# Pauses in the indexed transfers beside the first sorted tiles, and a PSUM tile for the last gates' values

## The chip, the core and the metric

The kernel runs on one core of a Trainium2 chip. The metric is the device time of one execution in microseconds (us); lower is better. Engines: PE (TensorE: matrix products and transposes), DVE (VectorE), ACT (ScalarE), POOL (GpSimd), SP (which issues most of the DMAs). SBUF is the working memory of 128 partitions, PSUM the small memory into which PE writes.

## What is computed

The input is `x`, four images of 32 x 128 x 128. Layer 0 groups pixels two by two, so that each image becomes a matrix `q` of 128 channels by 4096 positions:

```python
energy = einsum('bci,bcj->bij', q, q)          # 4096 x 4096 per image
energy = energy / (d_i * d_j)                  # d: root of the diagonal
out = gamma * einsum('bcj,bij->bci', q, softmax(energy)) + xs
```

Layer 1 sees each image as tokens of 128 values (4096 per image): a layer norm and a linear attention without softmax, added to the tokens, then a second layer norm and a mixture of eight experts, of which each token takes the best two:

```python
t = t + attention(ln(t))
probs = softmax(ln(t) @ router_w + router_b)
top_p, top_i = top_k(probs, 2); top_p /= sum(top_p)
t = t + sum_k top_p[k] * (ln(t) @ expert_w[top_i[k]] + expert_b)
```

## The kernel before

**Layer 0.** Images b = 0 to 3 follow each other in `attend` (L415). PE multiplies blocks of 128 x 512 of the normed `q` (L556), ACT takes the exponential (L559), PE multiplies the result with `q` transposed (L440). The matrix is symmetric, so a block's transpose serves the mirrored place; it is made by DVE, written to DRAM and read back by SP's DMAs (`blocks`, `G`), and used at L375 to L385. This loop fills PE for most of the time.

**Layer 1 as a stream.** The tokens of an image lie in SBUF as 32 rows of 128 tokens (`T`, `xn`: partition, row, value). `layer1(b)` returns generators whose every `yield` is one step. The main loop at the bottom walks through `attend`; it keeps a list `steady` and gives each stream in it one step every PACE = 10 units of the attention's clock, so layer 1 of image b runs inside the attention of image b + 1. On PE, DVE, ACT and SP the program's own order is kept (a manual schedule); an instruction that waits holds what stands behind it on its engine. POOL's power and indexed transfers are pinned in program order too.

For b = 0 to 2 a stream is `all_parts`: `close_rows` (ends layer 0's rows and makes the first norm's statistics, L690 on), `matrix` (the attention's small products), and `attention_rows`, which ends in `sorted_experts(h)` (L933 on) for the 16 rows of each half h. This sorts the tokens by expert:

- 32 indexed transfers, *scatters* (L989, issued by POOL), put each token's normed values at two places of a list `xs` in DRAM, two transfers per two steps. Half 1 starts its scatters when half 0's are issued (`turns[0]` has "moved").
- the list is read in pairs of tiles of 128 tokens by SP's DMAs (L1013, into `bufs`), transposed by PE (L1056), evicted by ACT (L1023), multiplied by the expert's weights on PE (L1049), evicted by DVE (L1032) and written to `ys` in DRAM (L1035).
- 32 indexed transfers, *gathers* (L1114, POOL), read the results back by token; DVE weighs and adds them (`combine`, L1083), SP stores the result. Half 0 gathers after half 1's scatters are issued, half 1 after half 0 gathered.

So half 1's scatters and half 0's first tiles are issued in the same steps. The first step of the next image's closing, `close_rows(0)`, waits until the stream before has finished its tiles (`st["sorted"]`).

**The last image.** After the attention there is nothing to hide behind. `last_parts` (L1186 on) therefore computes all eight experts for each token without sorting: two products of 128 x 512 per row k (L1198), DVE multiplying some experts by their gates and adding (`scaled_sums`, L1141), ACT scaling the others (`scaled_rows`, L1155; `by_scalar(k)` gives ACT 6 of 8 for k < 8, 5 for k < 14, else 4), POOL summing those (`sum_rows`, L1163 to L1167). The loop over k runs 32 + 4 times; each pass issues the products for row k + 2, and then one step of `rest`, the generator `second_half`: statistics of rows 16 to 31 (`close_stats`, L625 to L640), router (`router_rows`, L806 on), gates (`route(1)`, L821 on), normalising on ACT (L644) and transposes (`transpose_tokens`: PE L870, ACT copy L866). Rows 0 to 15 are routed before the loop; there the rows 8 to 15 are normalised and transposed too (8 ACT operations and tiles 2 and 3, before `for k`). Ahead of the loop stand `close_stats` of rows 0 to 15 with POOL's power `pow_neg_half` (L164), named `rsa` or `rsf` by its result.

PSUM's eight banks are shared out as two for `pe`, one `po`, two `pg`, three `pt` (`psum_t`).

Of the kernel before, what the change touches and what calls it, by code (L numbers as in the profile page):

```python
# [16 lines left out]
ALU = mybir.AluOpType  # L17
AX = mybir.AxisListType
# [4 lines left out]
def kernel(  # L23
# [43 lines left out]
    nc = tc.nc  # L67
# [11 lines left out]
    E = router_w.shape[1]  # L79
# [18 lines left out]
    def psum_t(name):  # L98
        return ps_t.tile([P, CH], F32, tag="pt", name=name)
# [6 lines left out]
    rank = const.tile([P, 1, E], F32, tag="rank", name="rank")  # L106
# [5 lines left out]
    rb_sb = const.tile([P, 1, E], F32, tag="rb", name="rb_sb")  # L112
# [3 lines left out]
    srw = const.tile([P, 1, E], F32, tag="srw", name="srw")  # L116
# [61 lines left out]
    def idle(n):  # L178
        for _ in range(2 * n):
            yield  # L180
# [421 lines left out]
    def layer1(b, st):  # L602
# [5 lines left out]
        rsf, nbf, nbo = (stat.tile([P, KT, 1], F32, tag=nm, name=f"{nm}_{b}", bufs=1) for nm in ("rsf", "nbf", "nbo"))  # L608
        lg = stat.tile([P, KT, E], F32, tag="lg", name=f"lg_{b}", bufs=1)
# [5 lines left out]
        gate = first  # L615
# [26 lines left out]
        def normalise(rows, rs, nb):  # L642
            for k in rows:
                nc.scalar.activation(xn[:, k, :], T[:, k, :], AF.Identity, scale=rs[:, k, :], bias=nb[:, k, :])  # L644
# [158 lines left out]
                    bank[:, ts(j - j0, D + 2 * E)], keep[k // 4][:, ts(k % 4, P)], matx, start=True, stop=True  # L803
                )

        def router_rows(eng, r0, nr, la):  # L806

            sh = [P, nr, E]
            rows = slice(r0, r0 + nr)
            w1, w2 = (stat.tile([P, 16, E], F32, tag=nm, name=f"{nm}_{b}_{r0}", bufs=1)[:, :nr] for nm in ("lw1", "lw2"))  # L810
            eng.tensor_tensor(w1, nba[:, rows].to_broadcast(sh), srw.to_broadcast(sh), ALU.mult)
            eng.tensor_tensor(w1, la[:, :, E:], w1, ALU.subtract)
            eng.tensor_tensor(w1, w1, sda[:, rows].to_broadcast(sh), ALU.mult)
            eng.tensor_tensor(w1, w1, la[:, :, :E], ALU.add)
            yield
            eng.tensor_tensor(w2, nbf[:, rows].to_broadcast(sh), srw.to_broadcast(sh), ALU.mult)
            eng.tensor_tensor(w2, w2, rb_sb.to_broadcast(sh), ALU.add)
            eng.tensor_tensor(w1, w1, rsf[:, rows].to_broadcast(sh), ALU.mult)
            eng.tensor_tensor(lg[:, rows], w1, w2, ALU.add)

        def route(h):  # L821

            sh = [P, KT // 2, E]
            rows = slice(h * KT // 2, (h + 1) * KT // 2)
            ms, dn = (stat.tile([P, KT // 2, 1], F32, tag=nm, name=f"{nm}_{b}_{h}") for nm in ("ms", "dn"))
            pr = stat.tile(sh, F32, tag="prob", name=f"prob_{b}_{h}", bufs=1)
            mx = weight[:, 1, rows]
            o1, o2 = first[:, rows], second[:, rows]
            v = lg[:, rows]
            nc.vector.tensor_reduce(mx, v, AX.X, ALU.max)  # L830
            nc.vector.tensor_tensor(pr, v, mx.to_broadcast(sh), ALU.subtract)
            nc.scalar.activation(pr, pr, AF.Exp)
            yield
            nc.vector.scalar_tensor_tensor(o1, pr, 1.0, rank.to_broadcast(sh), ALU.is_equal, ALU.mult)
            nc.vector.tensor_reduce(ms, o1, AX.X, ALU.max)
            nc.vector.tensor_tensor(o1, o1, ms.to_broadcast(sh), ALU.is_equal)
            nc.vector.scalar_tensor_tensor(pr, o1, -2.0, pr, ALU.mult, ALU.add)
            yield
            nc.vector.tensor_reduce(mx, pr, AX.X, ALU.max)
            nc.vector.tensor_tensor(o2, pr, mx.to_broadcast(sh), ALU.is_equal)  # L840
            nc.vector.tensor_tensor(o2, o2, rank.to_broadcast(sh), ALU.mult)
            nc.vector.tensor_reduce(ms, o2, AX.X, ALU.max)
            yield
            nc.vector.tensor_tensor(o2, o2, ms.to_broadcast(sh), ALU.is_equal)
            nc.vector.tensor_scalar(dn, mx, 1.0, None, ALU.add)
            nc.vector.reciprocal(dn, dn)
            if not alone:
                nc.vector.tensor_copy(weight[:, 0, rows], dn)
                nc.vector.tensor_tensor(mx, mx, dn, ALU.mult)
                return  # L850
            nc.vector.tensor_tensor(o2, o2, mx.to_broadcast(sh), ALU.mult)
            nc.vector.tensor_tensor(o1, o1, o2, ALU.add)
            nc.vector.tensor_tensor(gate[:, rows], o1, dn.to_broadcast(sh), ALU.mult)

        def add_rows(u, j0, la, pa):
            nj = min(3, 8 - j0)
# [5 lines left out]
        def transpose_tokens(g, alloc=psum_t):  # L862

            pt, done = hold(
                f"ptf_{b}_{g}",
                lambda p: nc.scalar.activation(xn[:, ts(g, 4), :], p.rearrange("p (j t) -> p j t", t=P), AF.Copy),  # L866
                alloc,
            )
            for j in range(4):
                nc.tensor.transpose(pt[:, ts(j, P)], xn[:, 4 * g + j, :], ident)  # L870
            return done
# [42 lines left out]
        def sorted_experts(h):  # L914


            sh = [P, HR, E]
            pad = HR // 2
            r0 = HR * h
            half = slice(r0, r0 + HR)  # L920
            o1, o2 = first[:, half], second[:, half]
# [65 lines left out]
            for n in range(2 * HR):  # L987
                k, i = r0 + n // 2, n % 2
                inst = nc.gpsimd.indirect_dma_start(xs[h], offset(place[:, i, k : k + 1]), xn[:, k, :], None)  # L989
                if not scatters:  # L990
                    pinned(inst)
                else:
                    tc.declare_no_dep(inst.ins, group=f"scatter_{b}_{h}", reason="no two tokens have the same place")
                tc.add_to_no_dep_group(f"scatter_{b}_{h}", inst.ins)
                wait_for(inst.ins, xs_made[h] + xs_read[h], "what is replaced was made and read before")
                wait_for(inst.ins, exps, "not more of these at a time than steps have")
                scatters.append(inst.ins)
                if n % 2:
                    yield
                    yield  # L1000
            turns[h].append("moved")
            xs_made[h][:], xs_read[h][:] = scatters, []
            yield from idle(3)
# [104 lines left out]
            for n in range(2 * HR):  # L1108
                k, i = r0 + n // 2, n % 2
# [59 lines left out]
        def store(g):  # L1169
            for s in range(2):  # L1170
                for r1 in range(2):
                    p0 = s * 64 + r1 * 32
                    nc.sync.dma_start(dst[s, r1, :, ts(g, 4), :], accs[g][p0 : p0 + 32])
# [9 lines left out]
        def last_parts():  # L1183
# [53 lines left out]
            def second_half():  # L1237

                bs, stats = batch_stats("f", 16, 16)
                for u in (2, 3):  # L1240
                    tg = T[:, ts(u, 8), :]
                    nc.vector.tensor_tensor(tg, tg, copies[u], ALU.add)
                    yield
                    for j in range(8):
                        stats[8 * u - 16 + j]()
                        if j % 4 == 3:
                            yield
                close_stats("f", 16, 16, bs)
                yield
                logits = router_rows(nc.vector, 16, 16, la[:, 16:])  # L1250
                next(logits)
                yield
                yield
                for _ in logits:
                    pass
                gates = route(1)
                next(gates)
                yield
                for g in range(4, 8):
                    normalise(range(4 * g, 4 * g + 4), rsf, nbo)  # L1260
                    next(gates, None)
                    yield
                    transpose_tokens(g)()
                    yield
# [10 lines left out]
            gates = route(0)  # L1275
# [4 lines left out]
                pass  # L1280
            products = [product(k, h, bank(f"py_{b}_{k}_{h}")) for k in range(2) for h in range(2)]
            transpose_tokens(1)()
            normalise(range(8, 16), rsf, nbo)
            transpose_tokens(2)()
            transpose_tokens(3)()
            for k in range(KT + 4):
                if k < KT:
                    n = by_scalar(k)
                    scaled_sums(k, products[:2], 8 - n)
                    scaled_rows(k, products[:2], n)  # L1290
                    products = products[2:]
                    if k + 2 < KT:
                        products += [product(k + 2, h, bank(f"py_{b}_{k + 2}_{h}")) for h in range(2)]
                if 1 <= k <= KT and k % 2 == 0:
                    sum_rows(k // 2 - 1, by_scalar(k - 2), nc.vector if k == KT else nc.gpsimd)
                if k >= 5 and k % 4 == 1:
                    store(k // 4 - 1)
                if k >= 1:
                    next(rest, None)

# [102 lines left out]
```

## Time and profile before

| | |
|---|---|
| three runs | 1736.75, 1737.0, 1741.14 us; median 1737.0 |
| profiled execution | 1730.18 us, of which the span of its instructions is 1728.4 |
| granted PE clock, mean | 0.989 |
| scatters L989 | 192, mean 0.969 us on POOL; 510.9-611.3, 924.5-1021.9, 1330.9-1428.3 |
| gathers L1114 | 192, mean 0.966 us; 660.0-772.3, 1072.6-1180.4, 1477.9-1583.1 |
| combines L1083 of image 2 | until 1588.9 |
| loop over k of the last image | about 1652.4 to 1723.4, last store landed at 1728.4 |

The profile records one execution. Its times count from the start of the span. A row of a timeline reads: start, duration, engine, line, operation, output<-inputs, shapes, how many in a row, and in brackets the idle time of the engine before it with what ended it ("<-ACT xn L1023": that instruction of ACT). Durations of L989 and L1114 are POOL's issuing; the transfer itself goes on in the DMA queues. A window table gives each engine's busy time within the stretch.

### The profile page before, as it was taken

Reading aid. Unit: us, or ns where it says so; the run is one execution under the profiler, and the core shown is the slowest. Engines: PE = TensorE matmul, PEld = TensorE weight load, DVE = VectorE, ACT = ScalarE, POOL = GpSimd, SP = SyncE. Lnnn points to the kernel's source line nnn. Section 1 sums busy time; section 2 is a strip of 40 time slices with the busy share of each in tenths; the row PEclk is TensorE's granted clock in tenths of the full one; section 3 lists DMA queues with packets and bytes.
Section 4 is the critical chain, followed back from the end, with each engine's and each line's share of the span. In section 5 each row is a group of like instructions: output and inputs, shape, how many; then the busy total and the mean of one; then the engine's idle time right before and its main releaser. Section 6 shows DMA issues by size and latency. Waiting matters only on the chain. (4 is left out here: it accounts for less than half of the span.)

```text
span 1728.4 us, 21211 instructions
## 1 busy us (share of the span) xinstructions
PE 1656.8 (96%) x5458; PEld 876.9 (51%) x5458; DVE 939.3 (54%) x2443; ACT 925.8 (54%) x2893; POOL 511.8 (30%) x553
## 2 busy tenths in 40 slices
PE   7999999999999999989999999999999999999887
PEld 4444444455554456445564455545555445544633
DVE  4433334367485235467568334557748524455686
ACT  3555445465565455446565544546656545545376
POOL 1000000011026514550014631652102650453156
PEclk9999999999999999989999999999999999999999
DMA  4775778876569899996568979998656988995001
GB/s 128 202 206 170 205 208 238 250 213 183 158 195 271 241 259 262 246 257 182 168 189 228 277 230 262 283 252 231 183 163 196 269 242 260 269 259 135 1 13 38
DMA packets 240681, 355.25 MB, mean 206 GB/s; under 512 B 27312, under 2 KB 155312, under 8 KB 226480
## 3 DMA queue, kind: packets, MB, share of 16 engines
q1 hardware_dynamic: 220048, 314.91, 64.5%
q0 software_dynamic: 12288, 25.19, 4.9%
q10 hardware_dynamic: 8224, 13.77, 2.8%
q8 instruction: 46, 0.75, 0.2%
q14 instruction: 75, 0.61, 0.1%
HBM read 183.64 MB, written 173.15 MB: 206 GB/s over the span
## 5 line engine op out<-in xcount | busy, mean ns | idle before, releaser
L559 ACT ACTIVATE pr<-pe 128x512 f32<-128x512 f32 (+1 forms) x576 | 322.4, 560 | 557.0 <-PE pe L556 428.8
L440 PE MATMUL po<-pr,qT 128*128 128x512 f32 (+3 forms) x1152 | 552.9, 562 | 3.9 <-ACT o L445 3.4
L375 PE MATMUL pg<-G,qT 128*128 128x512 f32 x880 | 453.4, 597 | 14.1 <-DMA G<-blocks 8.7
L556 PE MATMUL pe<-qn,qn 128*128 128x512 f32 x896 | 462.5, 598 | 3.3 <-ACT pr L559 3.0
L369 DVE STREAM_TRANSPOSE F<-pr 128x512 f32<-128x512 f32 x440 | 306.1, 702 | 156.1 <-ACT pr L559 132.1
L440 PEld LDWEIGHTS po<-pr,qT 128*128 128x128 f32 x1152 | 216.6, 191 | 251.8 <-issue 224.4
L380 ACT ACTIVATE junk<-G 128x512 bf16<-128x512 f32 x440 | 273.0, 621 | 7.1 <-DMA G<-blocks 7.0
L375 PEld LDWEIGHTS pg<-G,qT 128*128 128x128 f32 x880 | 167.5, 192 | 214.0 <-issue 187.0
L1114 POOL DMA_INDIRECT yb<-ys,place x192 | 185.5, 966 | 262.5 <-DMA xn<-xs 96.3
L989 POOL DMA_INDIRECT xs<-xn,place x192 | 186.1, 969 | 132.2 <-ACT pr L559 55.3
L556 PEld LDWEIGHTS pe<-qn,qn 128*128 128x128 f32 x896 | 155.3, 192 | 115.9 <-issue 103.0
L385 DVE TENSOR_TENSOR o<-o,pg 128x512 f32<-128x512 f32 x110 | 75.5, 686 | 203.1 <-PE pg L375 164.6
L164 POOL TENSOR_TENSOR rn<-ss,neg_half 128x8 f32<-128x8 f32 (+1 forms) x17 | 26.9, 1586 | 334.1 <-DVE ss L325 334.1
L559 ACT ACTIVATION_READ_ACCUMULATOR pr<-pe 128x1 f32 x576 | 112.1, 195 | 0.0
L1023 ACT ACTIVATE xn<-pys 128x256 f32<-128x256 f32 (+1 forms) x120 | 45.0, 377 | 118.3 <-PE pys L1056 67.7
L1049 PEld LDWEIGHTS pys<-ew_sb,xn 128*128 128x128 f32 x468 | 68.5, 192 | 56.3 <-issue 39.0
L164 POOL TENSOR_TENSOR rsf<-dm_f,neg_half 128x8 f32<-128x8 f32 (+1 forms) x15 | 26.2, 1748 | 233.7 <-DVE sv_f L636 233.7
L556 PE MATMUL pe<-qn 128*128 128x512 f32 (+3 forms) x256 | 91.1, 438 | 0.7 <-ACT qn L344 0.7
L164 POOL TENSOR_TENSOR rsa<-dm_a,neg_half 128x8 f32<-128x8 f32 x16 | 26.4, 1650 | 219.3 <-DVE sv_a L636 219.0
L380 ACT ACTIVATION_READ_ACCUMULATOR junk<-G 128x1 f32 x440 | 84.4, 192 | 0.0
L1049 PE MATMUL pys<-ew_sb,xn 128*128 x468 | 72.1, 277 | 11.1 <-ACT xn L1023 11.0
L1032 DVE COPY result<-pys 128x256 f32<-128x256 f32 (+1 forms) x60 | 24.6, 411 | 96.5 <-ACT xn L1023 48.7
(189 smaller groups left out, 1607.6 us busy)
## 6 DMA issues: line engine op xcount, KB each, us to landing
blocks<-F SPq DMA_DIRECT2D x108, 1024.0 KB
G<-blocks SPq DMA_DIRECT2D x432, 256.0 KB
xn<-xs SPq DMA_DIRECT2D x114, 128.0 KB
below<-F SPq DMA_DIRECT2D x31, 384.0 KB
G<-below SPq DMA_DIRECT2D x124, 96.0 KB
out_dram<-acc SPq DMA_DIRECT2D x128, 64.0 KB
xx<-in_x_dram SPq DMA_DIRECT2D x62, 128.0 KB
ys<-xn SPq DMA_DIRECT2D x60, 128.0 KB
```

The costliest lines, as they stand in the source:

```text
L164: pinned(nc.gpsimd.tensor_tensor(dst, src, neg_half.to_broadcast(list(src.shape)), ALU.pow))
L369: f()
L375: nc.tensor.matmul(pg.rearrange("p (a f) -> p a f", a=4), st["qT"][i][:, ib, :], G[:, :, ib], start=(ib == 0), stop=(ib == NJ - 1),)
L380: nc.scalar.activation(junk, G[:, :, ib], AF.Copy, accum_out=st["sums"][:, NJ * i + ib, jc : jc + 1])
L385: nc.vector.tensor_tensor(o, o, pg.rearrange("p (a j c) -> p a j c", a=4, c=S), ALU.add)
L440: nc.tensor.matmul(row["po"][:, lo:hi], qT[blk // NJ][:, blk % NJ, :], w, start=start, stop=(row["left"] == 0))
L556: nc.tensor.matmul(pe[:, c0:], qn[jc][:, ts(j, P)], qn[i][:, c0:], start=True, stop=True)
L559: nc.scalar.activation(pr[:, c0:], pe[:, c0:], AF.Exp, accum_out=sums[:, t, i : i + 1]).ins
L989: inst = nc.gpsimd.indirect_dma_start(xs[h], offset(place[:, i, k : k + 1]), xn[:, k, :], None)
L1023: nc.scalar.activation(bufs[4 + g % 2][:, :n], p[:, : n * P].rearrange("p (j t) -> p j t", t=P), AF.Copy)
L1049: nc.tensor.matmul(p[:, 2 * P + j * D : 2 * P + j * D + D], bufs[4 + g % 2][:, j, :], weights[:, bass.ds(begins[2 * (g % 2) + j], D)], sta ...
L1114: inst = nc.gpsimd.indirect_dma_start(yb[k // 4][:, i, k % 4, :], None, ys, offset(place[:, i, k : k + 1]))
```

## The change

1. In `sorted_experts`, half 1's scatters pause for `idle(2)`, which is four steps, after each eighth of the transfers n = 7, 15 and 23.
2. In the last image, `router_rows` and `route` take an optional PSUM tile `temps` of [128, 4, 16, 8], one `pt` bank. Rows 16 to 31 keep their intermediates there: one product, one sum and the logits (places 0 and 1), and in `route` the logits, the rank values, the probabilities and the second choice (0 to 3). About 20 DVE operations have at least one operand in PSUM instead of SBUF; the exponential's in and out lie there as well. Statistics, `dn` and the weights stay in SBUF.
3. The eight normalises of rows 8 to 15 and the transposes of tiles 2 and 3 move from before the loop over k into its passes 0 to 7: one row per pass, a tile's transposes and copy at passes 3 and 7, after that pass's products, scaled rows and sums, and before its step of `rest`.

The counts of instructions stay the same on PE, DVE and POOL.

```diff
-        def router_rows(eng, r0, nr, la):
+        def router_rows(eng, r0, nr, la, temps=None):
...
+            w0, sums = w2, lg[:, rows]
+            if temps is not None:
+                w1, w0, sums = temps[:, 0], temps[:, 1], temps[:, 0]
...
-            eng.tensor_tensor(w2, nbf[:, rows].to_broadcast(sh), srw.to_broadcast(sh), ALU.mult)
-            eng.tensor_tensor(w2, w2, rb_sb.to_broadcast(sh), ALU.add)
+            eng.tensor_tensor(w0, nbf[:, rows].to_broadcast(sh), srw.to_broadcast(sh), ALU.mult)
+            eng.tensor_tensor(w2, w0, rb_sb.to_broadcast(sh), ALU.add)
             eng.tensor_tensor(w1, w1, rsf[:, rows].to_broadcast(sh), ALU.mult)
-            eng.tensor_tensor(lg[:, rows], w1, w2, ALU.add)
-
-        def route(h):
+            eng.tensor_tensor(sums, w1, w2, ALU.add)
+
+        def route(h, temps=None):
...
+            ranks = o1
+            if temps is not None:
+                v, ranks, pr, o2 = (temps[:, n] for n in range(4))
...
-            nc.vector.tensor_tensor(o1, o1, o2, ALU.add)
-            nc.vector.tensor_tensor(gate[:, rows], o1, dn.to_broadcast(sh), ALU.mult)
+            nc.vector.tensor_tensor(o2, o1, o2, ALU.add)
+            nc.vector.tensor_tensor(gate[:, rows], o2, dn.to_broadcast(sh), ALU.mult)
...
                 if n % 2:
                     yield
                     yield
+                if h == 1 and n % 8 == 7 and n < 28:
+                    yield from idle(2)
...
-                logits = router_rows(nc.vector, 16, 16, la[:, 16:])
+
+                temps = psum_t("gates").rearrange("p (n k e) -> p n k e", n=4, e=E)
+                logits = router_rows(nc.vector, 16, 16, la[:, 16:], temps)
...
-                gates = route(1)
+                gates = route(1, temps)
...
-            normalise(range(8, 16), rsf, nbo)
-            transpose_tokens(2)()
-            transpose_tokens(3)()
...
+                if k < 8:
+                    normalise(range(8 + k, 9 + k), rsf, nbo)
+                    if k % 4 == 3:
+                        transpose_tokens(2 + k // 4)()
```

In `route` the rank operations use `ranks` in place of `o1` for their intermediate; `o1` itself stays in SBUF.

More of the change, by code (lines that the diff above doesn't have):

```diff
@@ L833, in route @@
             yield
-            nc.vector.scalar_tensor_tensor(o1, pr, 1.0, rank.to_broadcast(sh), ALU.is_equal, ALU.mult)
-            nc.vector.tensor_reduce(ms, o1, AX.X, ALU.max)
-            nc.vector.tensor_tensor(o1, o1, ms.to_broadcast(sh), ALU.is_equal)
+            nc.vector.scalar_tensor_tensor(ranks, pr, 1.0, rank.to_broadcast(sh), ALU.is_equal, ALU.mult)
+            nc.vector.tensor_reduce(ms, ranks, AX.X, ALU.max)
+            nc.vector.tensor_tensor(o1, ranks, ms.to_broadcast(sh), ALU.is_equal)
             nc.vector.scalar_tensor_tensor(pr, o1, -2.0, pr, ALU.mult, ALU.add)
```

## Prediction

> **What bounds the kernel now.** I read the page's shares first, then its chain of waits, then the timeline of the last 80 us, the timelines and windows around the first sorted tiles, and last how the change reorders each engine's instructions.
>
> ```profile
> PE 1656.8 (96%) x5458; PEld 876.9 (51%) x5458; DVE 939.3 (54%) x2443; ACT 925.8 (54%) x2893; POOL 511.8 (30%) x553
> ```
>
> TensorE is busy 1656.8 of 1728.4 us. What a change can give is among the 72 us in which it isn't, or where it stretches behind others. The chain has nothing but PE's lines at its head, so the question is local: where does PE stand still beside the edited lines? First place, the first sorted tiles of rows 0 to 15, in each of the batches 0 to 2 (batch 1 shown; the number in brackets is the engine's idle time before, with its releaser):
>
> ```profile
> 996.40 0.96 POOL L989 DMA_INDIRECT xs<-xn,place  x1 [0.30 <-issue]
> 999.48 0.39 ACT L1023 ACTIVATE xn<-pys 128x256 f32<-128x256 f32 x1 [6.50 <-remote]
> 999.91 0.71 PE L1049 MATMUL pys<-ew_sb,xn 128*128 x4 [3.36 <-ACT xn L1023]
> 1000.71 0.96 POOL L989 DMA_INDIRECT xs<-xn,place  x1 [3.35 <-ACT pr L559]
> ```
>
> The scatters run every 1.26 us (0.96 and 0.30 of issue) until 997.4. The first eviction of transposed tiles (L1023) then starts 6.50 us late, and the product behind it holds PE, in order, for 3.36 us. Two-microsecond windows (columns: length, busy time and count of PE, PEld, DVE, ACT, POOL, then PE clock, DMA share, GB/s):
>
> ```profile
> 991.00:993.00 2.00, 2.00 (x6) 0.95 (x5) 0.00 (x0) 1.45 (x5) 1.39 (x3) 1.00 1.01 423
> ...
> 995.00:997.00 2.00, 1.55 (x4) 0.38 (x2) 0.00 (x0) 0.00 (x0) 1.56 (x2) 1.00 0.21 72
> 997.00:999.00 2.00, 0.00 (x0) 0.00 (x0) 0.00 (x0) 0.00 (x0) 0.36 (x1) 1.00 0.10 33
> ```
>
> The DMA engines are full when the scatters and the sorted tiles' loads meet and empty while everyone waits. The last scattered packet lands at 998.49, and ACT is released 1 us later. The same place shows 3.74 us at 579.6 and 3.44 at 1402.9:
>
> ```profile
> 1406.33 0.71 PE L1049 MATMUL pys<-ew_sb,xn 128*128 x4 [3.44 <-ACT xn L1023]
> ```
>
> Rows 16 to 31 reach their first tiles with no scatter beside them, and the eviction there waits for PE alone, 1.08 us:
>
> ```profile
> 1434.96 0.38 ACT L1023 ACTIVATE xn<-pys 128x256 f32<-128x256 f32 x1 [1.08 <-PE pys L1056]
> ```
>
> Second place, the closing loop of batch 3 from 1652.43. ACT, not PE, sets its first 39.5 us: PE runs ahead by no more than its five banks.
>
> ```profile
> 1657.02 9.41 ACT L1155 ACTIVATE tmp<-py,first 128x128 f32<-128x128 f32 x36
> 1667.94 1.66 ACT L1155 ACTIVATE tmp<-py,first 128x128 f32<-128x128 f32 x6 [1.51 <-DVE acc L1141]
> 1675.87 0.31 ACT L832 ACTIVATE prob<-prob 128x128 f32<-128x128 f32 x1 [2.77 <-DVE prob L831]
> ...
> 1681.09 1.40 ACT L1155 ACTIVATE tmp<-py,first 128x128 f32<-128x128 f32 x5 [1.21 <-DVE acc L1141]
> ```
>
> ACT waits there for DVE, and DVE is late because small operations on SBUF stretch while POOL sums:
>
> ```profile
> 1672.25 1.90 POOL L1163 TENSOR_TENSOR tmp<-tmp 128x768 f32<-128x768 f32 x1
> 1672.40 1.90 DVE L818 TENSOR_TENSOR lw<-lw,rsf 128x128 f32<-128x128 f32 x1
> ```
>
> L818 takes as long as POOL's sum, although its usual time at half the size is 0.22. From 1697.94 on PE is without a gap (52 products in 22.58 us) and the rest, sums and stores to 1728.4, hangs on it; so time saved before 1697.9 moves the end one for one.
>
> **Part 1, the pauses.** Three pauses of four steps each in the scatters of rows 16 to 31 add no instruction. A step is 1.5 to 1.6 us, so these scatters end 17 to 19 us later in each of three batches, and their tiles, gathers (L1114) and combines (L1083) shift with them. What it can remove is 3.74 + 3.36 + 3.44 = 10.5 us of PE, bounded below by 0. [...] By the row, ACT starts 1 us after the last scattered packet in all three batches, and without scatters waits 1.08 us instead of 6.5. [...] The row is nearer, but a pause of four steps need not clear it: scatters still run between the pauses, and the loads still meet some. I take 0.7 of 10.5, 7.4 us.
>
> The cost is in batch 2. Before, its gathers end at 1583 and its combines at 1588.9. By the order of instructions, 14 of its gathers now stand on POOL ahead of batch 3's first power (rsa_3_0), where before 2 did, and 14 or more combines stand among batch 3's closing work on DVE, up to the last Gram product. That is 14 x 0.35 = 4.9 us more of DVE between 1589 and 1613, where DVE is nearly full from 1597.9 to 1606.8 and PE waits 2.10 for it. The POOL row is covered: rsa_3_0 ran at 1602.84 after 18.8 us of waiting for DVE, and the last gather comes at about 1583 + 19 = 1602. If the cover is gone, each us of lateness is a us of the end (rival D). I count 1.2 us, between 0 (combines fall in DVE's gaps) and 4.9 (none do). PE's other losses beside sorted work (about 11, 8 and 6 us in the stretches 720-780, 1140-1180, 1540-1580, where gathers and stores meet) move by a dozen steps; nothing says in which direction, so 0, bounds -3 and +3. Part 1: -7.4 + 1.2, about -6; bounds -10.5 and +5.
>
> **Part 2, the gates' values in a bank.** About 20 DVE operations of routing rows 16 to 31 (L811 to L852) get a PSUM operand. Two things pull apart. Cost: an elementwise operation with a PSUM operand takes 0.34 to 0.35 here (L1141, 106 of them), with SBUF alone 0.27 to 0.29: 20 x 0.07 = +1.4. [...] Gain: the excess of the stretched rows over their usual durations, L818 1.90, L834 1.62, L812 0.70, L819 0.77, L837 and L841 0.70 and the rest, sums to 6.7 us from L811 on (L633 and L635, 1.9 more, stay in SBUF). L1141, with its PSUM operand, is never stretched in the same stretch:
>
> ```profile
> L1141 DVE SCALAR_TENSOR_TENSOR acc<-py,first,acc x74: 349/351/353, 1653.0 to 1720.9; 128x128 f32<-128x128 f32 x74
> ```
>
> So the row decides: DVE falls by up to 6.7 - 1.4 = 5.3 us. What of it passes on is ACT's waiting.
>
> **Part 3, the normalising spread.** Before, ACT does 8 normalises (3.17) and the copies of two transposes ahead of its first scaled rows at 1657.02; now one normalise per k, copies at k = 3 and 7. ACT's work is the same; what changes is that DVE, PE and POOL start earlier and have slack when ACT needs them. Price: the two copies (ptf_2, ptf_3) now wait for PE's transposes in the loop, as the existing ones do, 0.68 each.
>
> **Parts 2 and 3 together**, by ACT from 1652.43 to 1691.97: 39.54 us, busy in the four windows 4.59 + 9.40 + 4.61 + 12.75 = 31.35, idle 8.2: waits for DVE 1.51 + 0.55 + 2.77 + 0.78 + 1.21 = 6.8 and for transposes 0.68 twice. After: four waits of 0.68 = 2.7 plus 0.8 left before the exponential. That is 3.5, so 8.2 - 3.5 = 4.7. PE needs 32.2 in this stretch (3.16 + 9.07 + 6.44 + 13.56) and DVE 33.1 - 5.3 = 27.8, both under 31.35 + 3.5, so neither takes over. I take -4.5; bounds -6 (ACT without the new waits) and 0. What is late next is PE: it was already gapless after 1697.9.
>
> **Sum.** -6 - 4.5 = -10.5. The profiled execution took 1730.18 (span 1728.4 and 1.8 around it) and would take 1719.7. The median of the runs shown, 1737.0, is 6.8 above it; the saving is the same: 1726.5.
>
> **Rivals.**
> A. The pauses don't take the stall away: the loads themselves, not the scatters, fill the DMA engines (share 1.01 at 991), or scatters between the pauses suffice. For it: [...] that the wait is marked "remote", a releaser the profile doesn't name. Against: the second half's 1.08. Then -4.5 alone, 1732.5.
> B. The bank and the spreading give nothing: PSUM's dearer operations and the two added waits eat what is freed, or POOL's stretching touches the operations left in SBUF (L845, L846). Against: ACT's listed 6.8 us of waits for DVE. Then part 1 alone, 1731.
> C. Both in full: the stall gone (-10.5), the loop -6, no cost: about 1720.5.
> D. Slower. Batch 2's last gathers are pushed into the closing stage beyond POOL's cover. If they end at 1612 instead of 1602, because a step is longer there or other transfers hold them, rsa_3_0 and its twin (before, 1602.84 and 1609.49) come some 9 us late and with them batch 3's normalising and everything behind it; with rival A at the first tiles: 1737 + 9.5 - 4.5 = 1742. It decides from the point where the last gather ends after 1609.5, and is against the 18.8 us that POOL waited there.
>
> **How the numbers follow.** Forecast 0.47 (1722 to 1730), A 0.17, B 0.13, C 0.14, D 0.09. About 0.3% of the time (5.2 us) is what a measurement can tell from no change. Faster by more: the forecast, C, and most of half of B with a little of A, 0.72; within: the rest of A and B, 0.20; slower: D, 0.08. The range leaves out D and the far end of C: 1719 to 1735.
>
> **What would show it.** Right, if in the profile after the first product L1049 of each first tile waits under 1.5 us, ACT's L1023 about 1 to 2 there, L818 and L834 take under 0.4, ACT's first scaled rows start about 4 us sooner after the loop's begin, and the gapless stretch of PE begins about 4.5 us sooner against the loop's start. Part 1 is wrong if the 3.4 us stand again, or turn up at another product; the cost is wrong if rsa_3_0 is released by POOL's own queue rather than DVE. The whole is wrong if PE's losses around the later gathers grow by more than the 10.5 us that the tiles can give.

## The result, and the profile after

Six runs after the change have a median of 1728.27 us (1724.84 to 1728.99), six of before 1736.88 (1734.24 to 1741.14): ratio 0.995, interval 0.9927 to 0.9974, or 8.7 us less (4.5 to 12.7). Forecast was 10.5 less. The profiled execution took 1726.51 us, span 1724.6, only 3.8 below the span before: the execution profiled before was the fastest of its kind by 4 us. The two traces therefore explain 3.8, not 8.7, and the rest of the account has to come from runs.

First the first sorted tiles in the profile after, batches 0 and 1 (line numbers move by 8: L1023 is L1031, L1049 is L1057, L1056 is L1064):

```profile
574.63 0.39 ACT L1031 ACTIVATE xn<-pys 128x256 f32<-128x256 f32 x1 [0.63 <-PE pys L1064]
...
577.00 0.61 PE L1057 MATMUL pys<-ew_sb,xn 128*128 x4
...
986.55 0.39 ACT L1031 ACTIVATE xn<-pys 128x256 f32<-128x256 f32 x1 [1.08 <-issue]
...
988.93 0.61 PE L1057 MATMUL pys<-ew_sb,xn 128*128 x4
```

These are the evictions that came late before: that of the first pair of tiles in batch 0, of the second pair in batches 1 and 2 (the first pair of batch 1 waited only 0.64 us before too, at 990.77). Waits of 6.48 and 6.50 us of ACT have become 0.63 and 1.08, and the products stand without a bracket: PE did not wait. The same holds in batch 2 (eviction at 1398.18, 1.08 us). All 10.5 us are gone. But ACT's releases marked "remote" turn up elsewhere. From the timeline after, beside the gathers and the closing stage of image 3:

```profile
1564.13 0.95 POOL L1122 DMA_INDIRECT yb<-ys,place  x1 [0.30 <-issue]
...
1568.38 0.60 ACT L537 ACTIVATE pr_back<-pe_back 128x512 f32<-128x512 f32 x1 [5.22 <-remote]
...
1569.12 2.08 PE L556 MATMUL pe<-qn,qn 128*128 128x512 f32 x2 [3.23 <-ACT pr_back L537]
...
1593.88 0.60 ACT L662 ACTIVATE xnT<-ptx 128x512 f32<-128x512 f32 x1 [7.28 <-remote]
...
1594.53 0.55 PE L466 MATMUL ptd<-ident,pr 128*128 128x128 f32 x3 [3.11 <-ACT xnT L662]
```

Now the closing loop after, from its timeline. The reader is to see ACT's scaled rows and normalises alternating without a bracket, the waits for transposes at 0.42 and 0.68, and one of DVE's operations (L821 was L818) at 0.30 beside POOL's sum:

```profile
1658.33 0.52 ACT L644 ACTIVATE xn<-T,nbo,rsf 128x128 f32<-128x128 f32 x1
1658.71 1.69 ACT L1163 ACTIVATE tmp<-py,first 128x128 f32<-128x128 f32 x6
...
1673.81 0.60 ACT L872 ACTIVATE xn<-ptf 128x512 f32<-128x512 f32 x1 [0.42 <-PE ptf L876]
1674.30 1.40 ACT L1163 ACTIVATE tmp<-py,first 128x128 f32<-128x128 f32 x5
1675.55 0.31 ACT L838 ACTIVATE gates<-gates 128x128 f32<-128x128 f32 x1
...
1672.35 1.81 POOL L1171 TENSOR_TENSOR tmp<-tmp 128x768 f32<-128x768 f32 x1
...
1672.62 0.30 DVE L821 TENSOR_TENSOR gates<-gates,rsf 128x128 f32<-128x128 f32 x1
```

Distances between events of PE, out of both traces, show where the two executions differ (us; "first tiles" is the first transpose of sorted tiles of a batch, the attention in the last two rows is that of layer 1, `pat`, L802 before):

| stretch | before | after | change |
|---|---|---|---|
| start to first tiles of batch 0 (nothing edited runs here) | 576.6 | 574.2 | -2.4 |
| to first tiles of batch 1 | 413.7 | 408.7 | -5.0 |
| to first tiles of batch 2 | 406.3 | 411.6 | +5.3 |
| to the last Gram product of batch 3 | 232.8 | 238.4 | +5.6 |
| to the last attention product | 13.7 | 13.7 | 0.0 |
| to the end | 85.2 | 77.9 | -7.3 |

The closing loop gave 7.3 us, more than was forecast. The three middle rows, which hold all three first tiles and everything that was moved, grew by 5.9: the 10.5 were won and some 16 lost again in this pair of executions.

### The profile page after: what moved, and what is told of

Same layout as the page of the kernel before. It is cut to its first block, busy times and chain, and to the rows that moved or that the text cites. A ratio compares the mean times of both kernels' runs of the same rounds, so it can differ in the third digit from the quotient of the medians.

```text
span 1724.6 us, 21171 instructions
## 1 busy us (share of the span) xinstructions
PE 1655.8 (96%) x5458; PEld 875.6 (51%) x5458; DVE 934.8 (54%) x2443; ACT 925.9 (54%) x2893; POOL 512.8 (30%) x553
## 5 line engine op out<-in xcount | busy, mean ns | idle before, releaser
L1031 ACT ACTIVATE xn<-pys 128x256 f32<-128x256 f32 x120 | 45.3, 378 | 113.3 <-PE pys L1064 64.4
L1057 PEld LDWEIGHTS pys<-ew_sb,xn 128*128 128x128 f32 x468 | 69.3, 191 | 53.2 <-issue 42.7
L1057 PE MATMUL pys<-ew_sb,xn 128*128 x468 | 72.2, 276 | 4.0 <-ACT xn L1031 3.8
```

The source lines that it names most:

```text
L1031: nc.scalar.activation(bufs[4 + g % 2][:, :n], p[:, : n * P].rearrange("p (j t) -> p j t", t=P), AF.Copy)
L1057: nc.tensor.matmul(p[:, 2 * P + j * D : 2 * P + j * D + D], bufs[4 + g % 2][:, j, :], weights[:, bass.ds(begins[2 * (g % 2) + j], D)], sta ...
```

## The experiments

All times are compared with runs of the kernel before on the same chip. The sets did not all run on one chip, which turned out to matter: before took 1717.7 and 1716.3 us in the first two sets, 1732.3 and 1731.2 in the last two, 1736.9 where before and after were first run.

**The parts alone.** `e1_pauses` has only the pauses; in `e2_bank` second_half calls both functions with `temps` and the rest is as before; `e3_spread` has only the normalises and transposes in the loop; `e4_tail` is the kernel after without

```diff
-                if h == 1 and n % 8 == 7 and n < 28:
-                    yield from idle(2)
```

> The three pauses alone, closing loop as before. Theory 1 (the pauses remove the wait at the first sorted tiles, part of it is lost again later): the 3.4 to 3.7 us before each first product L1049 gone, time 3 to 5 us below the kernel before. Theory 2 (they move the wait elsewhere, the whole gain comes from the closing loop): within 1.5 us of before. Theory 3 (the whole gain is the pauses'): 8 to 9 us below.

> The gates' values in a PSUM tile alone; no pauses, rows 8 to 15 normalised ahead of the loop as before. Theory 1 (DVE's small operations stop stretching beside POOL's sums, ACT's waits for DVE shrink): 1.5 to 3.5 us below before. Rival (PSUM operands cost more, or ACT's own work decides): within 1 us of before or up to 1.4 above.

> Only the normalises of rows 8 to 15 and the transposes of tiles 2 and 3 moved into the loop; no pauses, gates' values in SBUF as before. Theory 1 (DVE, PE and POOL begin 4 us earlier and ACT waits less): 2 to 4 us below before. Rival (ACT's work is the same and it only waits later, for the stretched operations of DVE): within 1 us of before.

> Both parts of the closing loop, no pauses. Theory 1 (closing loop 4.5 to 6 us, pauses the remaining 3 to 4): 4.5 to 6 us below before. Theory 2 (all gain is in the closing loop): 8 to 9 us below. Theory 3 (all gain is the pauses'): within 1 us of before. If the two parts add up, it is the sum of the bank's and the spread's own gains within 1 us.

| run | ratio, interval | us | last attention product to end |
|---|---|---|---|
| e1_pauses | 0.9957, 0.9946 to 0.9967 | -7.4 | 84.5 |
| e2_bank | 0.9957, 0.9943 to 0.9972 | -7.4 | 80.9 |
| e3_spread | 0.9981, 0.9971 to 0.9991 | -3.3 | 81.8 |
| e4_tail | 0.9962, 0.9951 to 0.9973 | -6.5 | 78.4 |

(us: the ratio's distance from 1, times the median before; the last column is of the profile and counts from the last `pat`.) The two parts of the loop nearly add up by the trace: 85.0 before (e5_before, below), less 4.0 with the bank, 3.1 with the spreading, 6.6 with both. Over all profiles this stretch is 84.3 to 86.4 us in the eight with the loop as before, 77.9 to 78.4 in the four with the loop as after. The whole time of e2_bank fell by more (4.8 to 9.8) than its loop, and by more than was expected of it; that is left open. e1_pauses won more than theory 1 gave it, and against the expectation not at the first tiles: the profiles of e2_bank, e3_spread and e4_tail, which have no pauses, show no such wait at all on this chip.

**Before again, after, and lateness without pauses.** `e5_before` and `e6_after` are the two kernels. `e7_shift` puts the twelve steps behind the scatters, `e8_half` halves the pauses:

```diff
+            if h == 1:
+                yield from idle(6)
             turns[h].append("moved")
```
```diff
-                    yield from idle(2)
+                    yield from idle(1)
```

> The kernel before, unchanged, for a second profile, taken on the chip that the other runs of this set use. If the wait at the first sorted tiles is the kernel's own, 3.4 to 3.7 us stand before each first product again. If it belongs to the chip of the first profile, they are missing, as in the kernels without pauses that ran before this one, and PE's losses are near 9 to 12 us in the stretches 720-760, 1120-1160 and 4 to 6 at 1520-1560. Time ratio 1.

> The kernel after, unchanged, beside its parts. If the pauses and the closing loop add up: 7.4 + 6.5 = 14 us below before. If they overlap or cost each other something (batch 2's late gathers in the closing stage): 8 to 10 us below, with PE's losses of the pauses alone at 1500-1600 growing.

> The pauses' twelve steps stand together behind the scatters of rows 16 to 31, ahead of the flag that lets the gathers go: the scatters run without a pause beside the first tiles, and everything after them comes as late as with the pauses; closing loop as before. Theory S (what counts is that the scatters are thinned beside the first tiles): nothing gained, within 1.5 us of before. Theory M (what counts is that gathers and the stores behind them come twelve steps later, clear of the next image's loads): 6 to 8 us below before.

> Three pauses of two steps instead of four, closing loop as before: the later work comes about 9 us later instead of 18. Theory S: most of the gain, 5 to 7 us below before. Theory M: it depends on whether the gathers are clear of the loads by then; half of the way, 2 to 5 us below before.

| run | ratio, interval | us |
|---|---|---|
| e5_before | 0.9996, 0.9986 to 1.0006 | -0.7 |
| e6_after | 0.9930, 0.9903 to 0.9957 | -12.0 |
| e7_shift | 0.9967, 0.9952 to 0.9981 | -5.7 |
| e8_half | 1.0046, 1.0027 to 1.0066 | +7.9 |

The kernel before, on this chip, at the same place with the same scatters:

```profile
980.25 0.96 POOL L989 DMA_INDIRECT xs<-xn,place  x1 [0.30 <-issue]
980.40 0.38 ACT L1023 ACTIVATE xn<-pys 128x256 f32<-128x256 f32 x1 [1.08 <-PE pys L1056]
...
982.78 0.61 PE L1049 MATMUL pys<-ew_sb,xn 128*128 x4
```

This is the second pair of batch 1, whose eviction waited 6.50 us in before; here it waits 1.08 and PE not at all. So the 6.5 us are not the kernel's own, they come and go with the set of runs (each later set had a chip of its own, so chip and set can't be told apart). e6_after's 12.0 agrees with the sum of the parts, 7.4 + 6.5 (interval 7.4 to 16.6). Of ACT's waits over 2.5 us with releaser "remote" there is none in the eight profiles of the first two sets. In before, after, e9_first_two, e10_third, e11_long and e12_both there are 5, 8, 7, 6, 2 and 5, of 26, 42, 34, 28, 12 and 26 us in all; beside all 33 of them POOL issued 2 to 5 indexed transfers, and 29 ended 1.1 to 2.2 us after the last of these.

The semaphore records of the traces show what was late. For each signal between engines (a semaphore) they hold the instruction that raises it and the time of the raise. All 33 waits ended with the semaphore that PE raises. Before the eviction at 999.48 in before, PE's last three instructions that raise it end at 993.98, 994.83 and 996.55, and the three raises stand together at 999.45 to 999.56; in e5_before each stands within 0.02 us of its instruction's end. Nor is it PE alone. Of the signals of PE, DVE and ACT in before that fall into stretches of indexed transfers (or up to 2.5 us behind one), 788 of 1699 have no record within 0.3 us of the instruction's end; of the 3365 outside these stretches, none. The other five profiles with "remote" waits look alike; each of the eight without has at most six such signals. What holds the signals back, and why on some chips only, stays open.

Where no such wait is to be had, the pauses still gain, by lateness: e7_shift, with no pause beside the tiles, keeps 5.7 of 7.4 (the intervals overlap). Lateness isn't good in itself, though: half of it lost 7.9, which neither theory foresaw. The stretch from the first tiles of batch 0 to the last Gram product shows where the time goes (us, one execution each; the last column is the stretch less PE's idle time and less half of its busy time at half clock, both from the trace; half, because in before products of 128 x 512 start 0.85 us apart at half clock and 0.43 at full, in the median):

| run | stretch | PE idle | PE busy at half clock | rest |
|---|---|---|---|---|
| e5_before | 1039.9 | 26.5 | 16.2 | 1005.4 |
| e1_pauses | 1034.1 | 24.4 | 6.3 | 1006.6 |
| e7_shift | 1036.7 | 25.8 | 9.6 | 1006.2 |
| e8_half | 1052.3 | 32.4 | 28.4 | 1005.8 |

The work is the same within 1.2 us. In these executions lateness gains mostly through the clock (5.0 us in e1_pauses, 3.3 in e7_shift) and less through idle time (2.1 and 0.7); half of the lateness loses about 6 by each. The profile of e8_half shows an example of either cost. Here is the first, in time order:

```profile
1561.45 6.30 SPq L476 DMA_DIRECT2D G<-F  x10
...
1567.86 4.02 SPq L1104 DMA_DIRECT2D out_dram<-acc  x8
...
1571.38 0.35 ACTq L1098 DMA_DIRECT2D acc<-t  x1
1572.09 1.65 ACT L644 ACTIVATE xn<-T,nba,rsa 128x128 f32<-128x128 f32 x4 [6.73 <-DMA yb<-ys,place]
1572.63 1.65 PE L676 MATMUL pgram<-xn 128*128 128x128 f32 x6 [4.32 <-ACT xn L644]
```

SP issues batch 2's stores only when its queue is through with image 3's loads; ACT's own queue holds the load L1098 of an `acc` tile, of which there are three, and everything of ACT stands behind it (6.73 us idle); then PE waits for ACT (4.32). No "remote" wait is involved. The semaphores show that the load waited for the stores: it waits for those of the first four, the last of which is raised at 1571.28. The gather in the bracket of L644 is only the last of several waits, at 1571.9. No run took the order of loads and stores apart. The second cost is the clock (window columns as before: PE busy is the second figure, the clock third from the end):

```profile
1570.00:1571.00 1.00, 0.00 (x0) 0.00 (x0) 0.00 (x0) 0.00 (x0) 0.70 (x2) 1.00 0.58 157
...
1573.00:1574.00 1.00, 1.00 (x6) 1.00 (x6) 0.00 (x0) 1.00 (x3) 0.00 (x0) 0.50 0.78 260
...
1577.00:1578.00 1.00, 1.00 (x3) 0.42 (x2) 0.00 (x0) 0.75 (x4) 0.59 (x1) 0.50 0.21 66
1578.00:1579.00 1.00, 1.00 (x3) 0.45 (x2) 0.00 (x0) 0.00 (x0) 0.69 (x2) 0.80 0.00 0
```

After 4.3 us of idleness PE works for 5.8 us at half its clock, which costs about 3 more (estimated as half of that time).

**Which image, and how late.** The chip of this set shows "remote" waits. `e9_first_two` adds `b < 2 and` to the pauses' condition, `e10_third` adds `b == 2 and`, `e11_long` has `idle(3)`; closing loop as before.

> The pauses of four steps in the images 0 and 1 only; closing loop as before. Theory M (later gathers and stores clear the next image's loads, about 1.3 to 3 us each): two of three shares, 3 to 5 us below before. If the gain belongs to the last image's closing stage: within 1.5 us of before.

> The pauses of four steps in image 2 only, whose later work meets the closing stage of image 3; closing loop as before. Theory M: 2 to 3 us below before. The forecast's charge for this place (combines among the closing work, +1.2, at a first tile that has no wait on this chip): 0 to 2 us above before.

> Three pauses of six steps, so that the later work comes about 27 us later. If lateness itself is what helps: more than the pauses of four steps, 8 to 10 us below before. If it is a matter of where stores and loads meet: less than they, anywhere between 5 below and 8 above before, with other waits of PE. Rival D of the forecast (the last gathers beyond POOL's cover): above before, with the power of image 3 released by POOL's own queue.

| run | ratio, interval | us |
|---|---|---|
| e9_first_two | 0.9980, 0.9967 to 0.9993 | -3.5 |
| e10_third | 1.0026, 1.0012 to 1.0041 | +4.5 |
| e11_long | 0.9997, 0.9983 to 1.0012 | -0.5 |

The wait at the first tiles follows the pauses exactly. In e9_first_two it stands only in batch 2, which has none:

```profile
1402.37 0.38 ACT L1031 ACTIVATE xn<-pys 128x256 f32<-128x256 f32 x1 [6.82 <-remote]
...
1402.81 0.71 PE L1057 MATMUL pys<-ew_sb,xn 128*128 x4 [3.64 <-ACT xn L1031]
```

In e10_third it is in batches 0 and 1 (2.92 and 1.59 us of PE) and not in batch 2; in e11_long nowhere. So on such a chip thinning the scatters does remove it. And yet the pauses of image 2 cost 4.5 us with their 3.4 to 3.6 already counted: about 8 us are lost behind them. In e10_third's profile PE's idle time from these tiles to the last Gram product, that wait left out, is 18.7 us against 13.2 in before, and two stretches of 3.4 us at half clock are new. Its gaps over 2 us that before lacks stand at 1481.9, at a gather, and at 1576.5 and 1591.7, where late gathers meet image 3's closing. Longer pauses show a part of rival D, POOL's power (of the first eight rows of image 3) directly behind the gathers:

```profile
1565.27 0.35 DVE L1091 SCALAR_TENSOR_TENSOR acc<-yb,weight,acc 128x128 f32<-128x128 f32 x1 [7.74 <-DMA yb<-ys,place]
...
1572.26 0.17 DVE L636 TENSOR_SCALAR sv_a<-sv_a 128x8 f32<-128x8 f32 x1
...
1576.95 0.95 POOL L1122 DMA_INDIRECT yb<-ys,place  x1 [0.30 <-issue]
1577.91 1.68 POOL L164 TENSOR_TENSOR rsa<-dm_a,neg_half 128x8 f32<-128x8 f32 x1
1579.67 0.20 POOL L638 TENSOR_TENSOR nba<-sv_a,rsa 128x8 f32<-128x8 f32 x1
1579.91 1.65 ACT L644 ACTIVATE xn<-T,nba,rsa 128x128 f32<-128x128 f32 x4 [14.82 <-issue]
...
1580.46 2.07 PE L676 MATMUL pgram<-xn 128*128 128x128 f32 x8 [12.40 <-ACT xn L644]
```

The power's input was ready at 1572.43, so 5.5 us of PE's 12.40 are the gathers ahead of the power on POOL. What came before is DVE's: it stood 7.74 us, until 1565.27, at a combine (L1091) that waited for a gather, with image 3's statistics behind it.

**The version that follows from it.** `e12_both` is the kernel after with `b < 2 and` in the pauses' condition.

> The kernel after, with the pauses in the images 0 and 1 only. If the pauses of image 2 cost what they did alone (4.5 us above before) and the closing loop brings its 6.5: 3.5 + 6.5 = 10 us below before on a chip that shows the late releases of ACT beside POOL's transfers (before near 1732), the waits at the first tiles of images 0 and 1 gone and that of image 2 back at 3.4 to 3.7 us. On a chip without such releases (before near 1716): no wait at the first tiles anywhere, 9 to 12 us below before.

Ratio 0.9924 (0.9899 to 0.9948), 13.2 us below before (9.0 to 17.5; 10 were expected); PE waits at the first tiles of batch 2 alone, 2.90 us, and the stretch from there to the last Gram product takes 235.7 us against 238.4 in after, although it holds this wait. It beats the kernel before. After was not run beside it on one chip: 0.9924 against 0.995, with overlapping intervals, speaks for it without settling it.

## Why the prediction was right, and where it wasn't

The total held (10.5 forecast, 8.7 measured), but by luck. The closing loop gave about 6.5 us instead of 4.5, which leaves some 2 of the 8.7 for the pauses, where 6 were forecast. And within the pauses two terms that were too small, of opposite sign, made up for each other. The forecast's own sign of being wrong, PE's losses around the later gathers growing by more than 10.5 us, was met in the two executions profiled: 10.5 won and 5.9 added make 16.

*The stall at the first tiles.* Forecast 7.4 of 10.5; all of it went, in after as in e9_first_two and e11_long. The row was right about what the pauses take away, but the reason given, DMA engines full of scatters and loads, did not hold: e5_before has the same transfers at the same place, nearly as dense (a scatter every 1.26 to 1.97 us instead of every 1.27), with more bytes moved in the 50 us around it (272 GB/s against 241), and no wait. What came late was PE's signal; ACT's copy itself took 0.39 us in before and 0.38 in e5_before. What is shown is that signals come late while POOL issues indexed transfers back to back (in before 788 of 1699), in three of the five sets of runs. The signs were there: "remote", and the DMA engines nearly idle within the wait. Three readings were off: the late eviction is the second pair's in batches 1 and 2; the last scattered packet ends at 998.27, 1.2 us ahead of ACT; and the row at 1434.96 belongs to rows 0 to 15, behind the scatters' end, not to rows 16 to 31. The 1.08 us that it shows stand beside scatters too, in e5_before.

*The cost of the later gathers.* This is the step that failed: the "1.2 us, between 0 (combines fall in DVE's gaps) and 4.9 (none do)" priced nothing but DVE's combines. In its place stand "remote" waits of 5.2 and 7.3 us of ACT in the closing stage (3.23 and 3.11 us of PE), and ahead of it others at gathers of all three batches. e10_third puts image 2's share at about 8 us. The forecast had bounds of 3 us for PE's other losses "by a dozen steps"; these were too narrow, and they depend on the chip: the same pauses are worth -7.4 without "remote" waits and about +1 (-3.5 and +4.5) with them. At eighteen steps combines did cost, but by DVE waiting in order for a gather (7.74 us) rather than by their own 0.35 us. The POOL row was moreover misread: the power at 1602.84, with its 18.8 us of slack, is that of image 3's second eight rows (rsa_3_8). The first, rsa_3_0, ran at 1579.27 in before, directly behind gathers and without any slack. The 14 gathers do not stand ahead of it either. In after it starts at 1577.07 and still waits for DVE (1.97 us), they come behind it, and rsa_3_8 at 1605.32 waits for DVE too (4.65): at twelve steps the cover held. At eighteen, rsa_3_0 was caught.

*The bank.* Forecast right in kind: the 24 small DVE operations of routing in the loop took 13.4 us before and 7.2 after, 6.2 less where 5.3 was forecast. They take 13.0 to 13.7 us in all nine profiles without the bank and 7.2 in all five with it. The four reductions among them, which read one tensor, were not stretched in before either (0.28 to 0.29). The extra price of a PSUM operand did not show: 0.29 to 0.30 against 0.28 to 0.29. L1141's 0.35, from which 0.07 was taken, is another operation. Operations left in SBUF still stretch (L632 1.84 us at 1664.57 after, 0.17 at half the size before the loop).

*The spreading.* ACT's scaled rows begin 3.7 us sooner, counted from the first product of the loop (6.78 instead of 10.45); forecast about 4. In e5_before they begin at 8.9, so about 1.5 of it hang on where a half-clock stretch fell; the loop was hardly shorter for it (0.3 us). Of ACT's 8.2 us of waiting 2.5 are left (0.31, 0.42, 0.42, 0.68, 0.68), where 3.5 was forecast: none before the exponential, and shorter ones for the two new transposes. So PE's last 52 products, without a gap in both, begin 6.7 us sooner (44.7 after the first product instead of 51.4), and the end follows: 7.3 by the trace (0.6 of it behind the last product), 6.6 and 6.5 by e4_tail, forecast 4.5. In e4_tail and e12_both the clock was never halved within the loop, in after and e6_after once, and the loop took as long: the clock is not the cause here.

*The rivals.* A, that the pauses don't take the wait away, fell on chips that have it. B, that the loop gives nothing, fell with e4_tail. C, both in full at no cost, fell with e10_third's 8 us. D did not decide, but its place, batch 2's gathers in image 3's closing, is where much of the gain was lost.

## What to carry to other kernels

A wait whose releaser is "remote" while the DMA engines are nearly idle is no property of the code until it has been seen in a second profile, if possible on another chip (here 6.50 us of ACT in before, 1.08 in e5_before); price it from both. Work that is moved later in an in-order stream is priced by what it meets at every later place, and not only at the one where it frees something: here six and twelve steps of lateness gave +7.9 and -7.4 us without "remote" waits, twelve and eighteen about +1 and -0.5 with them. Gaps of PE of two or three us are worth a look at the clock behind them (2.77 us in e5_before were followed by 3.4 at half clock). Short-lived elementwise chains are worth a PSUM tile while POOL works on SBUF (here 24 operations took 7.2 us instead of 13.4).

## What the runs showed of the hardware

The same kernel took 1716 to 1718 us in two sets and 1731 to 1737 in three, and the releases of ACT that come late beside POOL's indexed transfers, after waits of 2.8 to 7.3 us, are in the profiles of the latter only (26 us of ACT in the profile before). In these profiles about half of the signals of PE, DVE and ACT are recorded late or not at all within stretches of indexed transfers, and none elsewhere (788 of 1699 and 0 of 3365 in before). Packets of the DMA queues took as long in the one as in the other (81 against 80 ns in the mean on SP's queue).

A gap of PE can cost more than itself. After 2.77 us in e5_before the clock stood at half for 3.4 us; at a gap of 4.32 in e8_half for 6.8, of which 1.1 lie in the gap; at one of 12.4 in e11_long for 13.7, of which 8.7 lie in the gap; after 3.36 in before, not at all. In the clock records of before and after, the stretches at half clock last 3.41 us, two of before 6.83 (the last one of each trace runs past the end of the span), and their starts lie whole multiples of 3.413 us apart (the first two of before 153.6 us, 45 times that). What decides whether a gap is followed by such a stretch was not shown: one of 2.77 us was, one of 3.36 was not. PE worked at half clock behind these gaps for 3.4, 5.8 and 4.9 us, which by half of the time costs an estimated 1.7, 2.9 and 2.5 us on top of them.
